# Field-pair products on one core: loads moved to ScalarE's queue, stores of two pairs from three tiles

## The chip, the cores and the metric

The kernel runs on one core of a Trainium2 chip. The metric is device time in microseconds (us) of one execution. The engines are named as the profile names them: PE (TensorE matmul) and PEld (its weight load), DVE (VectorE), ACT (ScalarE), POOL (GpSimd) and SP (SyncE), whose only work here is to issue DMAs. A "q" behind an engine's name (SPq, ACTq) marks its instruction queue.

## The reference

```python
# inputs: r_inputs [1024, 32, 128], W [496, 128, 128], all float32
pairs = list(itertools.combinations(range(32), 2))          # 496 pairs (i, j), i < j
v_i = inputs[:, I_IDX, :]
v_j = inputs[:, J_IDX, :]
transformed = jnp.einsum('bpd,ped->bpe', v_i, W)
return transformed * v_j                                    # [1024, 496, 128]
```

As the subscripts stand, each pair p has a 128x128 matrix; field i's 1024 vectors go through it, and the result is multiplied element by element with field j's vectors. 260 MB of results go to HBM, and 49 MB of inputs and weights come from it.

## The kernel before, in words

The host only reorders: `xt` is [128 (d), 32 fields, 1024 samples], `wt` holds the matrices in 62 chunks of eight pairs (`WL` = 8), and the output is [496 pairs / `OG`, 128 (e), `OG`, 1024 samples]. Pairs are visited from field i = 30 down to 0 and j from i + 1 to 31, so that few fields are needed at the start.

A pair is worked in two halves of 512 samples (`HB`); such a half is a unit u, 992 in all. For the first 15 pairs (`nq0`, i from 30 to 26) `first(u)` is one plain float32 matmul from the raw weights. From there on the operands are split into high and low parts: `split_w(c)` cuts four pairs' weights (one ACT instruction on L92, three POOL instructions on L93 to L95) and `split_x(f, a)` half a field (L106 on ACT, L107 to L109 on POOL). Then `first(u)` is two matmuls (L148) and a scaling of the PSUM tile by ACT (L149). `second(u)` adds a third matmul (L157), and DVE multiplies the PSUM tile with field j into the output tile `ot` (L163).

One loop at the end writes out the order by hand (`manual_schedule`). At step u it does, in this order: every 16 units `load_w` of the chunk two ahead (`WLEAD`); at certain pairs `load_x` of two fields that are needed later (`XLEAD`); `first(u)`; `second(u - 3)` (`LAG` = 3); and at each odd u at most one split from the list `todo`, which is sorted by due time. Each engine runs its own instructions in this order. PSUM has 8 tiles `po`, so that PE can be at most eight units ahead of DVE.

The DMAs in question:

- **Stores.** Each pair has an `ot` tile of 4 KB in each partition, from a pool of six (L64, L162). After its second half SP issues the store of 512 KB (L167). The last two pairs go out in four halves (L165).
- **Weight loads** (L83): chunks of 512 KB, 4 KB in a row, into a pool of three tiles; all issued by SP. `load_w(4)` and those after it take over a tile that earlier splits on POOL, or matmuls, have read, and wait for these.
- **Field loads** (L74): fields 30 and 31 in four halves on ACT's queue, fields 29 and 28 and the pair 26/27 by SP before the loop, and from the loop 13 loads of two fields (1024 KB, rows of 8 KB), from 24/25 down to 0/1, all by SP.

SP handles its DMAs in program order, so a load in the loop stands between the stores of the pairs around it. The framework gives the DMAs eight semaphores in rotation in program order: a DMA also waits until the eighth one before it has landed.

Of the kernel before, what the change touches and what calls it, by code (L numbers as in the profile page):

```python
# [1 line left out]

# [4 lines left out]

F32 = mybir.dt.float32
F32R = mybir.dt.float32r
ALU = mybir.AluOpType  # L10

P = 128
NF = 32
NQ = NF * (NF - 1) // 2
BT = 1024
HB = 512
WC = 4
WL = 8
OG = 1
EPS = 2.0**-12  # L20
NATIVE = 5
LAG = 3
WLEAD = 2
XLEAD = 4


def _pairs():

    return [(i, j) for i in range(NF - 2, -1, -1) for j in range(i + 1, NF)]


@with_exitstack
def kernel(
    ctx: ExitStack,
    tc: tile.TileContext,
    xt: bass.AP,
    wt: bass.AP,
    out: bass.AP,
):

    nc = tc.nc
    pairs = _pairs()
    nchunk = NQ // WC

    xpool = ctx.enter_context(tc.tile_pool(name="x", bufs=1))  # L60
    spool = ctx.enter_context(tc.tile_pool(name="xs", bufs=2))
    rpool = ctx.enter_context(tc.tile_pool(name="wr", bufs=3))
    wpool = ctx.enter_context(tc.tile_pool(name="ws", bufs=3))
    opool = ctx.enter_context(tc.tile_pool(name="o", bufs=6))  # L64
    ppool = ctx.enter_context(tc.tile_pool(name="ps", bufs=8, space=bass.MemoryType.PSUM))

    x_sb = {}

    def load_x(f, n=1, pieces=1, eng=None):

        t = xpool.tile([P, n, BT], F32, tag=f"x{f}", name=f"x_{f}")
        s = BT // pieces
        for k in range(pieces):
            (eng or nc.sync).dma_start(out=t[:, :, k * s : (k + 1) * s], in_=xt[:, f : f + n, k * s : (k + 1) * s])  # L74
        for k in range(n):
            x_sb[f + k] = t[:, k, :]

    w_raw = {}

    def load_w(c, splits=(0, WL)):  # L80
        w_raw[c] = rpool.tile([P, WL, P], F32, tag="w", name=f"w_{c}")
        for a, b in zip(splits, splits[1:]):
            nc.sync.dma_start(out=w_raw[c][:, a:b, :], in_=wt[c, :, a:b, :])  # L83

    w_s = {}

    def split_w(c):

        k = c * WC % WL
        raw = w_raw[c * WC // WL][:, k : k + WC, :].rearrange("p q e -> p (q e)")  # L90
        h, l, d = [wpool.tile([P, WC * P], F32R, tag=t, name=f"{t}_{c}") for t in ("wh", "wl", "wd")]
        nc.scalar.mul(h, raw, 1.0 - 2.0**-13)  # L92
        nc.gpsimd.tensor_tensor(l, raw, h.bitcast(F32), ALU.subtract)  # L93
        nc.gpsimd.tensor_scalar(d, h.bitcast(F32), EPS, 1.0, ALU.mult, ALU.mult)  # L94
        nc.gpsimd.tensor_tensor(d, l.bitcast(F32), d.bitcast(F32), ALU.subtract)  # L95
        w_s[c] = (h, l, d)

    x_s = {}

    def split_x(f, a):  # L100

        if a == 0:
            x_s[f] = [spool.tile([P, BT], F32R, tag=t, name=f"{t}_{f}") for t in ("xh", "xl", "xd")]
        s = slice(a, a + HB)
        h, l, d = [t[:, s] for t in x_s[f]]
        nc.scalar.mul(h, x_sb[f][:, s], 1.0 - 2.0**-13)  # L106
        nc.gpsimd.tensor_tensor(l, x_sb[f][:, s], h.bitcast(F32), ALU.subtract)  # L107
        nc.gpsimd.tensor_scalar(l, l.bitcast(F32), 1.0 / EPS, 1.0, ALU.mult, ALU.mult)  # L108
        nc.gpsimd.tensor_tensor(d, h.bitcast(F32), l.bitcast(F32), ALU.subtract)  # L109

    nq0 = NATIVE * (NATIVE + 1) // 2
    c0 = nq0 // WC
    first_q = {i: q for q, (i, j) in reversed(list(enumerate(pairs)))}

    todo = []
    for c in range(c0, nchunk):
        todo.append(((c - 2) * WC + 1, max(c * WC, nq0), lambda c=c: split_w(c)))
    for i in range(NF - 2 - NATIVE, -1, -1):  # L120
        for a in range(0, BT, HB):
            todo.append((first_q[i + 1] + 1 if i < NF - 3 - NATIVE else 2, first_q[i], lambda i=i, a=a: split_x(i, a)))
    todo.sort(key=lambda t: t[1])

    load_w(0, (0, 1, WL))
    load_x(NF - 2, pieces=2, eng=nc.scalar)
    load_x(NF - 1, pieces=2, eng=nc.scalar)
    load_x(NF - 3)
    load_x(NF - 4)
    load_w(1)  # L130
    load_x(NF - 6, 2)


    ctx.enter_context(tc.manual_schedule())
    po, ots = {}, {}


    def first(u):
        q, h = divmod(u, 2)
        i, c = pairs[q][0], q // WC  # L140
        r = slice(q % WC * P, (q % WC + 1) * P)
        s = slice(h * HB, (h + 1) * HB)
        po[u] = ppool.tile([P, HB], F32, tag="po", name=f"po_{u}")
        if q < nq0:
            nc.tensor.matmul(po[u], w_raw[q // WL][:, q % WL, :], x_sb[i][:, s], start=True, stop=True)  # L145
        else:
            for t in (0, 1):
                nc.tensor.matmul(po[u], w_s[c][t][:, r], x_s[i][t][:, s], start=t == 0, stop=t == 1)  # L148
            nc.scalar.mul(po[u], po[u], 1.0 + EPS)  # L149

    def second(u):
        q, h = divmod(u, 2)
        i, j = pairs[q]
        r = slice(q % WC * P, (q % WC + 1) * P)
        s = slice(h * HB, (h + 1) * HB)
        if q >= nq0:
            nc.tensor.matmul(  # L157
                po[u], w_s[q // WC][2][:, r], x_s[i][2][:, s], start=False, stop=True, skip_group_check=True
            )
        g, k = divmod(q, OG)  # L160
        if k == 0 and h == 0:
            ots[g] = opool.tile([P, OG, BT], F32, tag="ot", name=f"ot_{g}")  # L162
        nc.vector.tensor_tensor(ots[g][:, k, s], po.pop(u), x_sb[j][:, s], ALU.mult)  # L163
        if q >= NQ - 2:
            nc.sync.dma_start(out=out[g, :, k, s], in_=ots[g][:, k, s])  # L165
        elif k == OG - 1 and h == 1:
            nc.sync.dma_start(out=out[g], in_=ots[g])  # L167

    for u in range(2 * NQ + LAG):
        q = u // 2  # L170
        if u % (2 * WL) == 0 and (q // WL + WLEAD) * WL < NQ:
            load_w(q // WL + WLEAD)
        if u < 2 * NQ:
            i, j = pairs[q]
            if u % 2 == 0 and j == i + 1 and i % 2 == 0 and 0 <= i - 2 - XLEAD:
                load_x(i - 2 - XLEAD, 2)
            first(u)
        if u >= LAG:
            second(u - LAG)
        if u % 2 == 1:  # L180
            ready = [t for t in todo if t[0] <= q]
            if ready:
                ready[0][2]()
                todo.remove(ready[0])
    assert not todo


# [25 lines left out]
```

## Time and profile before

| | |
|---|---|
| time, median of 8 runs | 781.26 us (779.21 to 783.45) |
| the profiled execution: its own time, its span | 779.21 us, 777.4 us |
| granted TensorE clock | 0.983 of full |
| PE / DVE / ACT / POOL busy | 711.0 / 631.2 / 617.1 / 549.7 us |
| HBM read / written | 49.28 / 260.05 MB |
| DMA packets | 83730, mean 399 GB/s |

The span runs from the first to the last instruction of the profiled execution; its own time is 1.8 us more. Busy times are those of one engine and overlap with the others'. Every DMA of this kernel is spread over 16 DMA engines, each of which moves eight of the 128 rows as one packet for a row and then sends a 4-byte packet for the semaphore. A transfer has landed when all 16 have done so. "Issue to landing" counts from the issue instruction to the last of the 16.

### The profile page before, as it was taken

The page shows a single profiled execution, that of the slowest core. Times are in us where ns is not written, and L with a number is a line of the kernel's source. Part 1 is how long each engine was busy: PE and PEld are TensorE (multiplying, and loading weights), DVE is VectorE, ACT ScalarE, POOL GpSimd, SP SyncE. Part 2 cuts the span into 40 slices and gives each one's busy share as a digit, 9 for nine tenths or more (in the row PEclk, how much of TensorE's full clock was granted, in tenths as well). Part 3 has the DMA queues.
Part 4 walks back from the last instruction along what each step waited for, and adds up shares of the span by engine and source line. Part 5 has one row for each costly group of instructions (what it writes and reads, how often), then busy time and mean ns, then how long its engine had stood idle before and what let it go on. Part 6 is the DMA issues. An engine that isn't in the chain of part 4 may idle for free.

```text
span 777.4 us, 11576 instructions
## 1 busy us (share of the span) xinstructions
PE 711.0 (91%) x2946; PEld 554.5 (71%) x2946; DVE 631.2 (81%) x992; ACT 617.1 (79%) x1136; POOL 549.7 (71%) x523
## 2 busy tenths in 40 slices
PE   7889889898998989998997999899999999999994
PEld 3477668686786867777775777677777777777773
DVE  4678769687897978878886898788988888889886
ACT  1289669797986987887886888688888888888883
POOL 0999898878687885876867586667676758585550
PEclk9999999999999999999999999999999999999998
DMA  9999999999999999999999999999999999999997
GB/s 354 419 379 414 408 377 396 398 407 394 413 410 407 411 404 418 392 405 412 410 399 395 388 397 389 402 408 395 395 414 400 397 403 399 408 408 396 406 415 314
DMA packets 83730, 310.10 MB, mean 399 GB/s; under 512 B 9296, under 2 KB 9424, under 8 KB 81872
## 3 DMA queue, kind: packets, MB, share of 16 engines
q1 hardware_dynamic: 83088, 308.32, 100.4%
q10 hardware_dynamic: 576, 1.05, 0.4%
q8 instruction: 23, 0.38, 0.2%
q14 instruction: 43, 0.35, 0.1%
HBM read 49.28 MB, written 260.05 MB: 398 GB/s over the span
## 4 chain that ended last, share of the span: by engine, by line
DMA 55%; DVE 22%; PE 19%; POOL 2%; issue 1%; DVEq 0%; SPq 0%; ACT 0%; POOLq 0%
DMA out_dram<-ot 52%; DVE ot L163 22%; PE po L148 13%; PE po L157 6%; DMA x<-in_xt_dram 2%; POOL xd L109 1%; POOL xl L107 1%; DMA w<-in_wt_dram 1%; DVEq L163 0%; POOL xl L108 0%; POOL wl L93 0%; SPq L83 0%; POOL wd L95 0%; ACT xh L106 0%; POOL wd L94 0%
## 5 line engine op out<-in xcount | busy, mean ns | idle before, releaser
L163 DVE TENSOR_TENSOR ot<-po,x 128x512 f32<-128x512 f32 x992 | 631.2, 686 | 139.1 <-DMA out_dram<-ot 105.2
L149 ACT ACTIVATE po<-po 128x512 f32<-128x512 f32 x962 | 539.5, 581 | 133.2 <-PE po L148 76.3
L148 PE MATMUL po<-xh,wh 128*128 128x512 f32 x962 | 385.9, 401 | 48.6 <-DVE ot L163 48.4
L148 PE MATMUL po<-xl,wl 128*128 128x512 f32 x962 | 379.6, 395 | 3.8 <-POOL wl L93 3.1
L157 PE MATMUL po<-xd,wd 128*128 128x512 f32 x962 | 378.3, 394 | 0.0
L93 POOL TENSOR_TENSOR wl<-w,wh 128x512 fp32r<-128x512 f32 x121 | 156.1, 1290 | 155.7 <-ACT wh L92 155.6
L148 PEld LDWEIGHTS po<-xh,wh 128*128 128x128 f32 x962 | 182.6, 190 | 113.9 <-DVE ot L163 74.7
L157 PEld LDWEIGHTS po<-xd,wd 128*128 128x128 f32 x962 | 183.0, 190 | 39.7 <-ACT po L149 0.4
L148 PEld LDWEIGHTS po<-xl,wl 128*128 128x128 f32 x962 | 182.8, 190 | 39.3 <-POOL wl L93 3.5
L95 POOL TENSOR_TENSOR wd<-wl,wd 128x512 fp32r<-128x512 f32 x121 | 156.4, 1292 | 10.1
L107 POOL TENSOR_TENSOR xl<-x,xh 128x512 fp32r<-128x512 f32 x52 | 67.2, 1292 | 22.5 <-ACT xh L106 22.5
L94 POOL TENSOR_SCALAR wd<-wh 128x512 fp32r<-128x512 f32 x121 | 74.8, 619 | 10.2
L92 ACT ACTIVATE wh<-w 128x512 fp32r<-128x512 f32 x121 | 75.7, 626 | 0.0
L109 POOL TENSOR_TENSOR xd<-xh,xl 128x512 fp32r<-128x512 f32 x52 | 67.0, 1289 | 4.3
L106 ACT ACTIVATE xh<-x 128x512 fp32r<-128x512 f32 x52 | 32.6, 630 | 14.0 <-DMA x<-in_xt_dram 14.0
L108 POOL TENSOR_SCALAR xl<-xl 128x512 fp32r<-128x512 f32 x52 | 32.2, 619 | 4.5
L145 PE MATMUL po<-x,w 128*128 128x512 f32 x60 | 27.9, 626 | 4.1 <-DMA x<-in_xt_dram 4.1
L145 PEld LDWEIGHTS po<-x,w 128*128 128x128 f32 x60 | 11.6, 198 | 19.7 <-issue 12.8
L106 ACT ACT_TABLE_LOAD x1 | 1.3, 1283 | 2.6 <-issue 2.6
L200 POOL MEMSET const-float32-0.0<- 128x1 f32 x1 | 0.1, 98 | 0.2 <-issue 0.2
L200 POOL MEMSET const-bfloat16-1.0<- 128x1 bf16 x1 | 0.1, 101 | 0.0
L200 POOL MEMSET const-uint8-127<- 128x1 uint8 x1 | 0.1, 101 | 0.0
(1 smaller groups left out, 0.1 us busy)
## 6 DMA issues: line engine op xcount, KB each, us to landing
out_dram<-ot SPq DMA_DIRECT2D x494, 512.0 KB, 7.6
w<-in_wt_dram SPq DMA_DIRECT2D x61, 512.0 KB, 7.2
x<-in_xt_dram SPq DMA_DIRECT2D x14, 1024.0 KB, 10.1
x<-in_xt_dram ACTq DMA_DIRECT2D x4, 256.0 KB, 5.6
x<-in_xt_dram SPq DMA_DIRECT2D x2, 512.0 KB, 6.8
out_dram<-ot SPq DMA_DIRECT2D x4, 256.0 KB, 6.1
w<-in_wt_dram SPq DMA_DIRECT2D x1, 448.0 KB, 4.5
w<-in_wt_dram SPq DMA_DIRECT2D x1, 64.0 KB, 3.1
```

The lines of the kernel that those rows point to most:

```text
L92: nc.scalar.mul(h, raw, 1.0 - 2.0**-13)
L93: nc.gpsimd.tensor_tensor(l, raw, h.bitcast(F32), ALU.subtract)
L94: nc.gpsimd.tensor_scalar(d, h.bitcast(F32), EPS, 1.0, ALU.mult, ALU.mult)
L95: nc.gpsimd.tensor_tensor(d, l.bitcast(F32), d.bitcast(F32), ALU.subtract)
L106: nc.scalar.mul(h, x_sb[f][:, s], 1.0 - 2.0**-13)
L107: nc.gpsimd.tensor_tensor(l, x_sb[f][:, s], h.bitcast(F32), ALU.subtract)
L109: nc.gpsimd.tensor_tensor(d, h.bitcast(F32), l.bitcast(F32), ALU.subtract)
L145: nc.tensor.matmul(po[u], w_raw[q // WL][:, q % WL, :], x_sb[i][:, s], start=True, stop=True)
L148: nc.tensor.matmul(po[u], w_s[c][t][:, r], x_s[i][t][:, s], start=t == 0, stop=t == 1)
L149: nc.scalar.mul(po[u], po[u], 1.0 + EPS)
L157: nc.tensor.matmul(po[u], w_s[q // WC][2][:, r], x_s[i][2][:, s], start=False, stop=True, skip_group_check=True)
L163: nc.vector.tensor_tensor(ots[g][:, k, s], po.pop(u), x_sb[j][:, s], ALU.mult)
```

## The change

`OG` goes from 1 to 2 and the pool of output tiles from six to three: an `ot` tile now holds two pairs, 8 KB in each partition, and is stored by one DMA of 1024 KB after its fourth unit. The output array is [248, 128, 2, 1024], so that each row of a store is 8 KB in one piece. The bytes of the pool and of the output are the same. The last two pairs still go out in four DMAs of 256 KB.

The loads in the loop (60 of weights, 13 of fields) are issued by ACT on its own queue in place of SP. What is loaded before the loop stays where it was: `eng` says so at each call.

```diff
-OG = 1
+OG = 2
...
-    opool = ctx.enter_context(tc.tile_pool(name="o", bufs=6))
+    opool = ctx.enter_context(tc.tile_pool(name="o", bufs=3))
...
     def load_x(f, n=1, pieces=1, eng=None):
...
-            (eng or nc.sync).dma_start(out=t[:, :, k * s : (k + 1) * s], in_=xt[:, f : f + n, k * s : (k + 1) * s])
+            (eng or nc.scalar).dma_start(out=t[:, :, k * s : (k + 1) * s], in_=xt[:, f : f + n, k * s : (k + 1) * s])
...
-    def load_w(c, splits=(0, WL)):
+    def load_w(c, splits=(0, WL), eng=None):
...
-            nc.sync.dma_start(out=w_raw[c][:, a:b, :], in_=wt[c, :, a:b, :])
+            (eng or nc.scalar).dma_start(out=w_raw[c][:, a:b, :], in_=wt[c, :, a:b, :])
...
-    load_w(0, (0, 1, WL))
-    load_x(NF - 2, pieces=2, eng=nc.scalar)
-    load_x(NF - 1, pieces=2, eng=nc.scalar)
-    load_x(NF - 3)
-    load_x(NF - 4)
-    load_w(1)
-    load_x(NF - 6, 2)
+    load_w(0, (0, 1, WL), nc.sync)
+    load_x(NF - 2, pieces=2)
+    load_x(NF - 1, pieces=2)
+    load_x(NF - 3, eng=nc.sync)
+    load_x(NF - 4, eng=nc.sync)
+    load_w(1, eng=nc.sync)
+    load_x(NF - 6, 2, eng=nc.sync)
...
-        if q >= NQ - 2:
+        if q >= NQ - OG:
             nc.sync.dma_start(out=out[g, :, k, s], in_=ots[g][:, k, s])
         elif k == OG - 1 and h == 1:
             nc.sync.dma_start(out=out[g], in_=ots[g])
```

## The prediction, made before the changed kernel ran

> **What bounds the kernel now.** I read the page's engine rows, its DMA rows and its chain first, then the table of waits, then the DMA answer for single stretches.
>
> ```profile
> PE 711.0 (91%) x2946; PEld 554.5 (71%) x2946; DVE 631.2 (81%) x992; ACT 617.1 (79%) x1136; POOL 549.7 (71%) x523
> ...
> DMA packets 83730, 310.10 MB, mean 399 GB/s; under 512 B 9296, under 2 KB 9424, under 8 KB 81872
> ...
> q1 hardware_dynamic: 83088, 308.32, 100.4%
> ...
> DMA 55%; DVE 22%; PE 19%; POOL 2%; issue 1%; DVEq 0%; SPq 0%; ACT 0%; POOLq 0%
> ```
>
> The DMA engines are busy from end to end (100.4%: neighbouring packets overlap by 3 to 4 ns in the records), and the chain that ended last is mostly stores. The waits say the same:
>
> ```profile
> POOL wl L93 <- ACT wh L92: 155.6, 67, 4.7
> DVE ot L163 <- DMA out_dram<-ot: 105.2, 65, 5.0
> ACT po L149 <- PE po L148: 76.3, 69, 4.2
> ...
> PE po L148 <- DVE ot L163: 48.4, 48, 3.6
> ...
> PEld po L157 <- ACT po L149: 0.4, 1, 0.4
> ```
>
> DVE waits for an output tile, PE for DVE. ACT is waited for once, for 0.4 us. SP's own table has 459.3 us of waiting for DVE: its issue slots are no limit. Yet PE is close behind: between 500 and 700 us it is busy 95.5% of the time, ACT 86.1%.
>
> Two stretches give prices: 23 to 29 us moves stores alone, 594 to 600 us has a weight load among them.
>
> ```profile
> DMA packets 691, 2.52 MB, mean 420 GB/s; under 512 B 76, under 2 KB 76, under 8 KB 691
> ```
> ```profile
> DMA packets 634, 2.31 MB, mean 384 GB/s; under 512 B 71, under 2 KB 71, under 8 KB 634
> ```
>
> At 420 GB/s a transfer of 524,288 bytes takes 1.248 us. The DMA answer for 500 to 735 us has 160 stores and 20 weight loads: 180 x 1.248 = 224.6 of 235 us. The other 10.4 us are 0.52 us for each load beyond its own bytes.
>
> **Larger packets.** In the packet records a 4 KB packet takes 159 ns and its successor starts 155.3 ns after it; for 8 KB it is 309 and 306 ns, for a semaphore packet 6 ns. A 1 MB store is 8 x 306 + 6 = 2.454 us on each engine, two of today's are 2.496. That spares 0.042 us x 247 = 10.4 us, if the DMA stays the bound. The row that shows 8 KB packets is that of the field loads (14 x 128 of the 1858 packets of 8 KB and more); stores with such rows are not in the trace. Bounds: 0 if writes to HBM set the pace, 10.4 if it is the packet. I take 10.4, as 4 KB loads and stores show the same 159 ns.
>
> The Trainium skill bears on this: "DMA: Bandwidth & Descriptors", section "Rules for kernel authors", wants at least 1 MiB in a DMA, and its section "Anatomy of one DMA" gives 2.0 us fixed for each (on GpSimd's path). By that alone 247 fewer DMAs would spare an estimated 494 us. The stores-only row (420 GB/s at 512 KB) contradicts it here: fixed parts lie beside other transfers.
>
> **Loads on ACT's queue.** 60 weight and 13 field loads leave SP, which gains nothing (459.3 us spare). Each becomes an instruction of ACT:
>
> ```profile
> L83 SPq DMA_DIRECT2D w<-in_wt_dram x63: 328/667/1104, 0.7 to 735.0; - x63
> ```
> ```profile
> L74 SPq DMA_DIRECT2D x<-in_xt_dram x16: 424/1112/1487, 1.6 to 478.7; - x16
> ```
>
> (ns: least, median, most.) At the least it is 60 x 0.328 + 13 x 0.424 = 25 us, by medians 54 us, at most 86 us; ACT goes from 617 to between 642 and 703 us. Behind the issue stand the scaling (L149) of the next units and the splits, and for the scaling waits PE's third matmul. The cover is the lag of three units (a PE unit is 0.68 us, so 2.0 us) against an issue and a split (0.626 us) in a row, and PE's idle time: eight pairs take 11.75 us (235 / 20) and PE needs 16 x 0.68 = 10.9 us. I cost the issues at nothing; uncovered, 54 us. In a queue of their own loads also no longer stand in line behind stores; as the DMA engines are the bound, this moves bytes about but removes none.
>
> The skill's section "Issuing engines are not separate DMA queues" on the same page says so too: issuing from several engines saves sequencer time only. The sum would be the same by it, except that it leaves ACT's cost out.
>
> **The start.** `load_w(4)` waits for a split on POOL: SP waited 6.1 us for it (POOL wl L93), until 39.64 us. Now ACT waits, while its scalings began at 36.89 us: up to 2.8 us late, and PE and DVE with it, while the DMA ran dry (0.94 busy between 40 and 45 us). Against this, the load of fields 24/25 (issued at 6.11, landed at 17.85 us) no longer stands behind 2 MB of SP's loads, and POOL's chain could begin 2 us earlier. Bounds -2 to +2.8, taken +1. Other moved loads reuse tiles that were read long before, and the eighth DMA back is a store that must have landed for DVE to be where ACT's position implies: no wait.
>
> **Three tiles for six.** This is what the change may cost. Today, without queueing, a tile's round is 1.30 us of filling (two DVE instructions), 0.15 us to the issue, and 2.48 us from issue to the arrival from the fastest engine (least over all stores, from the sixteen semaphore arrivals of each): 3.9 us. Six stores keep an engine busy for 7.5 us: a cushion of 3.6 us. Changed: 2.60 + 0.15 + 2.48 + 1.21 (the longer data) = 6.4 us against 3 x 2.454 = 7.4: a cushion of 0.9 us, or 2.2 when a weight load (1.25 us) falls into the round. The cushion is used now: from 500 to 735 us the last of the 16 arrivals comes 2.4 us after the ninth (median). Engines that met slow load packets fall behind, the others work ahead; with a short cushion they idle, and each load's delay on the worst engine counts instead of the mean. Bounds for the 73 moved loads: nothing, to the same 0.52 us once more, 38 us. I take what the spread exceeds the cushion by in a load's round, 2.4 - 2.2 = 0.2 us: 73 x 0.2 = 14.6 us.
>
> **The sum.** -10.4 + 0 + 1 + 14.6 = +5.2 us on the span of 777.4: 782.6; 1.8 us around it: 784.4. The profiled execution (779.21) lies 2.05 us under the median of the runs: 786.4 us. A change below 0.2% (1.6 us) can't be told from none here.
>
> **The rivals.**
> - *The cushion suffices.* For it: even 0.9 us is positive, and loads arrive as extra work just when they disturb. Against it: the spread of 2.4 us. 781.26 - 10.4 + 1 = 771.9 us; with part of the 38 us of load stretches gone, since loads now mix with stores, down to 765. It wins while the cushion costs under 7.8 us, 0.11 us a load. Chance 0.36.
> - *It cancels*, cushion cost 7.8 to 11: 780 to 782.8, so 781.3 us. Chance 0.09.
> - *ACT holds PE up.* PE has 0.85 us spare in eight pairs; an issue over that (the longest was 1.10) makes PE the bound: 62 x 0.25 = 16 us for weights, and 13 x 1.49 = 19 us for field loads with nothing spare beside them, and no gain from packets: 781.3 + 35 + 1 = 817 us; half of that, about 799, is likelier. For it: PE at 95.5%. Against it: ACT's first four issues took 0.41 to 0.45 us on an empty queue. Chance 0.12.
> - *The change not doing what it says* (8 KB rows cut in two) is excluded by the field loads' packets.
>
> **How the numbers follow.** The forecast, 0.43, is the short cushion: from 782.8 up to 781.26 - 10.4 + 1 + 38 = 810. Slower is this and the third rival, 0.55. The range for 8 in 10 starts at 768, leaving out the rival's luckiest end, and stops at 807.
>
> **What would show it.** Right: "DVE ot <- DMA out_dram" stays the largest wait of DVE, some 42,000 data packets, 8 KB at 309 ns, the DMA's share under 100% with holes between loads, and a smaller gap from ninth to last arrival. Packets at 309 ns with the DMA full and the span near 768 would be the first rival; "PEld L157 <- ACT" growing from 0.4 to tens of us the third. If 8 KB stores take over 318 ns, the first step is wrong.

## The result, and the profile after

The changed kernel takes 792.61 us (median of 11 runs, 789.03 to 796.58) against 781.59 us (32 runs of the kernel before): a ratio of 1.0143, 95% interval 1.0124 to 1.0163. It is slower, as forecast, but by 11 us where 5 were forecast. The profiled execution took 788.23 us with a span of 786.4 us; its counterpart before had 779.21 and 777.4. Ratios leave out executions more than 1.5% above the fastest of the same kernel: one of six in e3, and in the kernel of e1 and e10, whose 24 executions lie between 776 and 800 us, nine of twelve and two of twelve.

The DMA rows and the chain of the page after:

```profile
DMA packets 48156, 310.03 MB, mean 394 GB/s; under 512 B 5344, under 2 KB 5472, under 8 KB 14688
...
q1 hardware_dynamic: 37008, 263.21, 81.3%
q10 hardware_dynamic: 11088, 46.14, 17.4%
...
DMA 42%; PE 30%; DVE 22%; POOL 4%; issue 1%; DVEq 0%; ACT 0%; ACTq 0%; POOLq 0%
```

The packets fell from 83730 to 48156 and 33,468 of them now have 8 KB or more: the change did what it says. The two queues together fill 98.7% of the DMA engines' time where one filled 100.4%, and the mean rate fell from 399 to 394 GB/s though the packets are cheaper. PE's share of the chain rose from 19 to 30%: over more of the span it was not a store that was waited for, but the next product.

The table of waits after:

```profile
DVE ot L163 <- DMA out_dram<-ot: 107.2, 63, 4.9
...
ACT po L149 <- PE po L148: 77.1, 69, 10.9
PE po L148 <- DVE ot L163: 51.7, 50, 3.4
DVE ot L163 <- PE po L157: 25.6, 27, 2.2
...
PE po L157 <- ACT po L149: 0.9, 1, 0.9
...
PEld po L157 <- ACT po L149: 0.4, 1, 0.4
```

DVE still waits for stores most, and for about as long as before (105.2). What grew is DVE's wait for PE's third matmul, from 7.9 to 25.6 us; the row before was:

```profile
DVE ot L163 <- PE po L157: 7.9, 10, 1.3
```

PE hardly waits for ACT (0.9 us, its weight load 0.4). ACT's issues by line:

```profile
L83 ACTq DMA_DIRECT2D w<-in_wt_dram x60: 334/334/369, 3.9 to 744.9; - x60
```
```profile
L74 ACTq DMA_DIRECT2D x<-in_xt_dram x17: 334/335/1216, 0.7 to 486.0; - x17
```

On ACT an issue takes 0.334 us, half of what SP's weight loads took (0.667); this queue holds loads alone.

**A budget of the DMA engines** makes the kernels comparable. From the packet records of each trace, as a mean of the 16 engines: *work* is the number of packets of each size times the distance of their starts when nothing is in the way (4 KB 155.3 ns, 8 KB 306, semaphore 6); *slow* is what packets took beyond their usual duration (159 and 309 ns); *idle* is the rest of the span, less some 2.5 us of instruction fetches.

| kernel (profiled execution) | span | work | slow | idle |
|---|---|---|---|---|
| before | 777.4 | 736.3 | 28.9 | 9.8 |
| after | 786.4 | 725.4 | 41.1 | 17.6 |

The larger packets gave 10.9 us. Slow packets took 12.2 back and idle time 7.8; the sum is the 9.0 us between the two spans.

### The profile page after: what moved, and what is told of

The parts are those of the page before. It is cut to its first block, busy times and chain, and to the rows that moved or that the text cites. A ratio compares the mean times of both kernels' runs of the same rounds, so it can differ in the third digit from the quotient of the medians.

```text
span 786.4 us, 10835 instructions
## 1 busy us (share of the span) xinstructions
PE 718.4 (91%) x2946; PEld 557.5 (71%) x2946; DVE 618.1 (79%) x992; ACT 624.9 (79%) x1136; POOL 549.9 (70%) x523
## 2 busy tenths in 40 slices
DMA packets 48156, 310.03 MB, mean 394 GB/s; under 512 B 5344, under 2 KB 5472, under 8 KB 14688
## 4 chain that ended last, share of the span: by engine, by line
DMA 42%; PE 30%; DVE 22%; POOL 4%; issue 1%; DVEq 0%; ACT 0%; ACTq 0%; POOLq 0%
DMA out_dram<-ot 39%; DVE ot L163 22%; PE po L148 21%; PE po L157 10%; DMA x<-in_xt_dram 2%; POOL xl L107 1%; POOL xd L109 1%; POOL wl L93 1%; POOL wd L95 0%; POOL xl L108 0%; DVEq L163 0%; POOL wd L94 0%; ACT xh L106 0%; ACT wh L92 0%; ACT po L149 0%
## 5 line engine op out<-in xcount | busy, mean ns | idle before, releaser
L163 DVE TENSOR_TENSOR ot<-po,x 128x512 f32<-128x512 f32 x992 | 618.1, 684 | 162.2 <-DMA out_dram<-ot 107.2
L149 ACT ACTIVATE po<-po 128x512 f32<-128x512 f32 x962 | 543.7, 581 | 135.2 <-PE po L148 77.1
L95 POOL TENSOR_TENSOR wd<-wl,wd 128x512 fp32r<-128x512 f32 x121 | 156.3, 1292 | 10.1
L94 POOL TENSOR_SCALAR wd<-wh 128x512 fp32r<-128x512 f32 x121 | 74.9, 619 | 10.2
L92 ACT ACTIVATE wh<-w 128x512 fp32r<-128x512 f32 x121 | 75.8, 627 | 0.8 <-PE po L145 0.8
L109 POOL TENSOR_TENSOR xd<-xh,xl 128x512 fp32r<-128x512 f32 x52 | 66.9, 1286 | 4.3
L106 ACT ACTIVATE xh<-x 128x512 fp32r<-128x512 f32 x52 | 32.6, 630 | 10.9 <-DMA x<-in_xt_dram 10.9
L145 PEld LDWEIGHTS po<-x,w 128*128 128x128 f32 x60 | 12.0, 207 | 20.8 <-issue 14.6
```

## The experiments

Theory 1: three tiles of two pairs leave the DMA engines too little queued work (the cushion of the prediction), so that they run dry and packets get slow. Rival 2: the loads on a queue of their own do it. Rival 3: a store of 1 MB with 8 KB rows is slow in itself. All ratios are against the kernel before on the same chip.

**e1 and e10: the loads alone.**

```diff
 (the changed kernel, with)
-OG = 2                        bufs=3
+OG = 1                        bufs=6
```

> One part of the change alone: the loop's loads on ScalarE's queue, stores as before (one pair, six tiles). Theory 1 (short cushion: the loss comes from three output tiles in place of six): no change within 0.4%, 779 to 785 us, the only cost being the start, about +1 us; DVE still waits some 105 us for stores. Rival 2 (queue: loads on a queue of their own mix with the stores on every DMA engine and make packets slow, or ScalarE holds TensorE up): slower by 0.8 to 1.5%, 788 to 793 us, with the time of load packets beyond 159 ns (4 KB) and 309 ns (8 KB) well above the 28 us (mean of an engine) that before has.

> The loads on ScalarE's queue alone, once more, since the twelve runs of the first time lay between 778 and 800 us. Theory 1: 779 to 785 us. Rival 2 (queue): 788 to 793 us. If the kernel has two ways of running, both will show again.

Measured: 0.9984 (0.9957 to 1.0011), and again 0.9989 (0.9960 to 1.0018), in the profile of e10 (776.84 us) with slow packets of 24.9 and 11.4 us idle. In the executions that the ratios compare, the loads' queue alone changes nothing. But the 0.9984 rests on three executions of e1, the median of all twelve is 791.0 us (781.71 in e10), and the one profiled in e1 (797.63 us) has 39.1 us of slow packets and 18 idle, as much as the changed kernel, with six small tiles. So e1 and e10 don't settle rival 2; e2 and e6 below do. Why the executions of this kernel scatter is open.

**e2: the stores alone.**

```diff
 (the kernel before, with)
-OG = 1                        bufs=6
+OG = 2                        bufs=3
```

> The other part alone: stores of two pairs with 8 KB rows from three tiles, loads on SyncE as before. Theory 1 (short cushion): as slow as the full change or slower, 790 to 797 us, DMA engines idle for 10 us or more between 30 and 765 us. Rival 2 (queue): the packets' 10 us are gained and nothing is lost, 770 to 774 us. Rival 3 (an 8 KB store is slower in itself): 790 to 797 us too, but with 8 KB store packets over 318 ns where no load is near.

Measured: 798.09 us, 1.0238 (1.0203 to 1.0273), a little above the expected 790 to 797; slow 46.1, idle 22.8 us. So the stores alone bring a loss, and without the queue of the loads it is larger: 1.0238 against 1.0143.

**e3: four small tiles.**

```diff
-    opool = ctx.enter_context(tc.tile_pool(name="o", bufs=6))
+    opool = ctx.enter_context(tc.tile_pool(name="o", bufs=4))
```

> The kernel before with four output tiles in place of six, nothing else (4 KB rows, loads on SyncE). By the prediction's arithmetic its cushion is 4 x 1.248 - 3.9 = 1.1 us, close to the 0.9 us of the full change, and no packet is saved. Theory 1 (short cushion): slower by 2 to 3%, 797 to 804 us (the 22 us that the full change lost, without its 10 us of gain). Rivals 2 and 3 (queue; large stores): no change, 780 to 783 us.

Measured: 857.92 us, 1.0971 (1.0936 to 1.1006). No large store and no moved load is in it, so fewer tiles cost time by themselves. The waits of this kernel show where:

```profile
DVE ot L163 <- DMA out_dram<-ot: 185.9, 82, 6.2
...
PE po L148 <- DVE ot L163: 108.3, 64, 5.2
```

82 waits for a store in all, a little over one for each of the 73 loads of the loop, and 2.3 us long on the mean (185.9 / 82) where before has 1.6 (105.2 / 65). The budget: work 736.3 as before, slow 62.3, idle 52.7. The direction is theory 1's, the size is not: 77 us were lost where 16 to 23 were expected. The cushion as the prediction computes it (1.1 us here, 0.9 in the changed kernel) does not rank these two kernels. Part of the difference may be the queue, for e3 has its loads on SP; but e2, which has them there too, lost less as well (1.0238).

**e4: each pair of a tile stored on its own.**

```diff
-        elif k == OG - 1 and h == 1:
-            nc.sync.dma_start(out=out[g], in_=ots[g])
+        elif h == 1:
+            nc.sync.dma_start(out=out[g, :, k, :], in_=ots[g][:, k, :])
```

> The full change, but each pair of a tile is stored on its own as soon as it is done: 512 KB DMAs, 4 KB rows, still three tiles of two pairs, loads on ScalarE. The first pair's store starts two units earlier; cushion 5 x 1.248 - 3.9 = 2.3 us in place of 0.9, the packets' 10 us not gained. Theory 1 (short cushion): 784 to 790 us, faster than the full change though its packets are small. Rival 2 (queue): the full change's loss without its gain, 800 to 804 us. Rival 3 (large stores slow in themselves): 780 to 783 us.

Measured: 788.34 us, 1.0102 (1.0078 to 1.0126). It is no slower than the full change although it gives up its gain (the intervals just touch): slow 37.5, idle 11.6, work 736.3 us. That the first pair's store starts two units earlier is worth at least about as much as the larger packets.

**e5, e6, e7: more tiles, with one load left out to make room.**

```diff
     def load_x(f, n=1, pieces=1, eng=None):
+        if f == 0:
+            x_sb[0], x_sb[1] = x_sb[2], x_sb[3]
+            return
 (e5: the changed kernel;  e6: the same with bufs=4;  e7: the kernel before with bufs=8)
```

> Control for the next run: the full change, with the load of fields 0 and 1 left out (fields 2 and 3 stand in for them), which frees 8 KB of each partition. One load of 1 MB less is some 2.5 us of DMA time plus its slow packets. All theories: 1.0 to 1.2% slower than before, 787 to 791 us.

> The control with four tiles of two pairs in the freed memory, nothing else changed. The cushion goes from 0.9 to 0.9 + 2.45 = 3.4 us, nearly the 3.6 us of six small tiles. Theory 1 (short cushion: it makes the DMA engines run dry and makes load packets slow): the packets' 10.9 us come out, 1.2 to 1.9% faster than before, 766 to 772 us; idle time of the DMA engines back from 17.6 to about 10 us and slow packets from 41 to about 29 us. Rival 2 (loads on their own queue cost): as the control less a little, 783 to 790 us. Rival 3 (large stores slow in themselves): as the control, 787 to 791 us.

> The kernel before with eight tiles of one pair and the load of fields 0 and 1 left out; cushion 8 x 1.248 - 3.9 = 6.1 us. It shows whether six small tiles were themselves short. Theory 1, if a cushion of 3.6 us covers the spread of 2.4 us: only the load left out counts, 777 to 779 us. If slow packets go on falling with a longer cushion: 768 to 774 us. Rivals 2 and 3 say nothing of it beyond 777 to 779 us.

Measured: e5 789.22 us, 1.0101 (1.0085 to 1.0116); e6 760.80 us, 0.9740 (0.9725 to 0.9755); e7 775.16 us, 0.9928 (0.9905 to 0.9951). One more tile of two pairs takes 28 us off, more than expected. The DMA rows of e5 and, below it, of e6:

```profile
DMA packets 48012, 308.98 MB, mean 392 GB/s; under 512 B 5328, under 2 KB 5456, under 8 KB 14672
```
```profile
DMA packets 48012, 308.98 MB, mean 407 GB/s; under 512 B 5328, under 2 KB 5456, under 8 KB 14672
```

The same packets, 392 and 407 GB/s. Slow fell from 39.7 to 22.6 us and idle from 22.5 to 10.6. Rivals 2 and 3 fall here: the queue and the store are the same in both. In e7 eight small tiles gain some 3 us beyond the load left out (slow 26.0). That doesn't show that six were nearly enough, for eight tiles were not free to queue up in e7. SP's own table of waits has a row there that before does not have (L169 is the store):

```profile
SPq L169 <- DMA out_dram<-ot: 238.9, 340, 2.3
```

With eight semaphores in rotation a store is issued only when the eighth DMA before it has landed, and 340 times that was another store.

**e9: four large tiles, the loads back on SP.**

```diff
 (the kernel before, load of fields 0 and 1 left out, with)
-OG = 1                        bufs=6
+OG = 2                        bufs=4
```

> Four tiles of two pairs, the load of fields 0 and 1 left out, and the other loads of the loop on SyncE as before: what the queue is worth once the cushion is long. Theory 1 (short cushion), with the queue as a side matter: 760 to 765 us, within 0.5% of the run with the loads on ScalarE (760.8 us). If the queue of their own is what keeps slow packets low (22.6 us there against 28.9 before): 766 to 772 us with slow packets near 29 us.

Measured: 767.60 us, 0.9817 (0.9796 to 0.9839); slow 28.9, idle 11.1. The second of the two expectations came true. Against e6 (0.9740) the loads' own queue is worth 0.8%, nearly all of it in slow packets: 28.9 against 22.6 us. With large tiles it helps at either length of cushion (e2 and the full change, e9 and e6). With small ones the ratios of e1 and e10 show no gain; slow packets fell there too (28.9 to 24.9 us in e10), but idle time rose (9.8 to 11.4). SP's table of e10 has two rows that bear on this:

```profile
SPq L167 <- DMA w<-in_wt_dram: 84.4, 39, 3.5
SPq L167 <- DMA x<-in_xt_dram: 23.2, 8, 4.0
```

A store needs nothing from a load, but it takes over the semaphore of the eighth DMA before it, and here that was often a load that had not landed: 107.6 us in all. In the kernel before it was 15.8 us, in those with stores of 1024 KB between 0 and 16.1 us. Whether these waits ate up the gain was not tried.

**e8 and e11: complete kernels with four large tiles.** The pool needs 8 KB more, which come from elsewhere:

```diff
 (both, from the changed kernel)
-    opool = ctx.enter_context(tc.tile_pool(name="o", bufs=3))
+    opool = ctx.enter_context(tc.tile_pool(name="o", bufs=4))
+    wpool2 = ctx.enter_context(tc.tile_pool(name="ws2", bufs=2))     # holds wl and wd
 (e8)
-    rpool = ctx.enter_context(tc.tile_pool(name="wr", bufs=3))
+    rpool = ctx.enter_context(tc.tile_pool(name="wr", bufs=2))
-        if u % (2 * WL) == 0 and (q // WL + WLEAD) * WL < NQ:
+        if u % (2 * WL) == WL and (q // WL + WLEAD) * WL < NQ:
 (e11)
-                load_x(i - 2 - XLEAD, 2)
+                if i - 2 - XLEAD:
+                    load_x(i - 2 - XLEAD, 2)
+                else:
+                    load_x(1)
+            if u == 2 * first_q[1] - 8:
+                t = rpool.tile([P, WL, P], F32, tag="w", name="x_0").rearrange("p q e -> p (q e)")
+                nc.scalar.dma_start(out=t, in_=xt[:, 0, :])
+                x_sb[0] = t
```

> A complete kernel with four tiles of two pairs. The memory comes from two raw weight tiles in place of three (each load of weights four pairs later) and two tiles each of wl and wd in place of three; the rest is the full change. Theory 1 (short cushion): 768 to 775 us, faster than both kernels, unless ScalarE or GpSimd now wait for tiles; the waits would show that. Rivals 2 and 3: 785 to 793 us.

> A second complete kernel with four tiles of two pairs, which keeps three raw weight tiles and the times of the weight loads: the memory comes from two tiles each of wl and wd in place of three, and from field 0, which is loaded late into a raw weight tile. Theory 1: the idle time at the start that the first one had (17.5 us in all) falls to about 11 us: 762 to 767 us. If GpSimd's waits for wl and wd tiles are what held the first one back: 768 to 772 us.

Measured: e8 769.84 us, 0.9862 (0.9841 to 0.9883); e11 767.95 us, 0.9812 (0.9791 to 0.9834). Both beat both kernels. The rows of e11, and its waits (its lines stand one lower: L94 and L95 are the POOL instructions for wl and wd, L149 and L158 the matmuls, L164 the product):

```profile
PE 713.4 (93%) x2946; PEld 555.0 (72%) x2946; DVE 625.9 (82%) x992; ACT 618.5 (81%) x1136; POOL 551.1 (72%) x523
...
DMA packets 48300, 310.03 MB, mean 404 GB/s; under 512 B 5360, under 2 KB 5488, under 8 KB 14960
```

```profile
POOL wd L95 <- PE po L158: 74.8, 76, 2.2
DVE ot L164 <- DMA out_dram<-ot: 69.2, 69, 3.0
...
POOL wl L94 <- PE po L149: 50.9, 35, 5.1
```

DVE's wait for stores is down from 107.2 to 69.2 us. POOL now waits for its smaller pools (74.8 and 50.9 us), and PE waits 18.1 us for POOL's L94 and L109 (10.7 and 7.4) where the changed kernel has 2.9. Slow 26.4, idle 12.6 us. e11 lies at the edge between its two expectations (762 to 767 and 768 to 772), so it doesn't tell whether POOL's waits held e8 back.

All budgets but that of e1, in us of a mean DMA engine, in the order of slow and idle together:

| kernel | output tiles x pairs | loads on | work | slow | idle | ratio |
|---|---|---|---|---|---|---|
| e6 (a load less) | 4 x 2 | ACT | 722.9 | 22.6 | 10.6 | 0.9740 |
| e10 | 6 x 1 | ACT | 736.3 | 24.9 | 11.4 | 0.9989 |
| e7 (a load less) | 8 x 1 | SP | 733.8 | 26.0 | 11.9 | 0.9928 |
| before | 6 x 1 | SP | 736.3 | 28.9 | 9.8 | 1 |
| e11 | 4 x 2 | ACT | 725.4 | 26.4 | 12.6 | 0.9812 |
| e9 (a load less) | 4 x 2 | SP | 722.9 | 28.9 | 11.1 | 0.9817 |
| e8 | 4 x 2 | ACT | 725.4 | 23.0 | 17.5 | 0.9862 |
| e4 | 3 x 2, stored by pair | ACT | 736.3 | 37.5 | 11.6 | 1.0102 |
| after | 3 x 2 | ACT | 725.4 | 41.1 | 17.6 | 1.0143 |
| e5 (a load less) | 3 x 2 | ACT | 722.9 | 39.7 | 22.5 | 1.0101 |
| e2 | 3 x 2 | SP | 725.4 | 46.1 | 22.8 | 1.0238 |
| e3 | 4 x 1 | SP | 736.3 | 62.3 | 52.7 | 1.0971 |

## Why the prediction was wrong in size and right in direction

- **Larger packets, -10.4 us: right.** Work fell by 10.9 us, and the usual 8 KB store packet took 309 ns, like the loads of before (316.8 on the mean, with the slow ones). The signs named for it (some 42,000 data packets, 8 KB at 309 ns) are there: 48156 - 5344 = 42,812. So are three others: "DVE ot <- DMA out_dram" is DVE's largest wait, the DMA's share is under 100%, and the gap from the ninth to the last arrival shrank.
- **ACT's issues, nothing: right.** 60 x 0.334 + 13 x 0.335 = 24.4 us, a little under the lower bound of 25, and PE waited 0.9 us for ACT, its weight load 0.4. The third rival is refuted. (The sentence that ACT is waited for once holds for PE alone; POOL waited 155.6 us for ACT's L92, as the first row of that table says.)
- **The start, +1 us: right within its bounds.** Slow and idle time of the first 60 us rose from 5.1 to 7.1 us, 2.0 where the bounds were -2 and 2.8. The half that was to be gained failed: ACT's first split began at 18.52 us, not earlier than the 17.88 of before; and the scalings after `load_w(4)` began at 40.69, 3.8 us later than before.
- **Three tiles for six, +14.6 us: the mis-sized term.** With the start taken out it measured 18 us: slow and idle rose by 20.0 in all, slow packets by 12.2 and idle time by 7.8. The step that failed is the line "I take what the spread exceeds the cushion by in a load's round, 2.4 - 2.2 = 0.2 us". It treats the spread as a fixed demand and a load's slow packets as a fixed price. The runs show neither. The spread shrank from 2.4 to 0.67 us (last arrival after the ninth, stores from 500 to 740 us), though the prediction itself names a smaller gap as a sign; with four large tiles it was 3.0 to 3.2 us (e11, e6). With 0.67 us the same line would have charged nothing, so that 14.6 came near 18 is luck. And slow packets depend on how much is queued: in the table above, with the same loads but for the one left out in some runs, they cost 22.6 to 28.9 us with long queues and 37.5 to 62.3 with short ones. (The one profiled in e1, 39.1 us with six small tiles, doesn't fit, and stays open.) I had put a load's price once more into the upper bound (38 us) and then took a number from the spread of the old profile. The runs support about 0.25 us for a moved load (18.0 / 73) in place of 0.2.
- **The rest of the miss.** The sum was -10.4 + 1 + 14.6 = +5.2; between the profiled executions it was +9.0, and the medians differ by 11.0, since the profiled execution of the changed kernel lies 4.4 us under its median and that of before 2.4. The terms explain 9 of the 11 us; the last two are a difference of runs that no profile here resolves. The forecast was a small difference of two large terms: 3.4 us too little for the tiles and 1.0 for the start, less the 0.5 that the packets gained beyond the forecast, make 3.9 of the 5.8 us by which the medians miss it.
- **The first rival** (the cushion suffices) is refuted by e2 and e6 together: the gain it promised comes out with a fourth tile and not with three. The second (it cancels) is refuted by the ratio, whose interval starts at 1.0124.
- **What the cushion lacks** is open in one point. By its formula e3 (1.1 us) should have lost as much as the changed kernel (0.9 us), but slow and idle rose by 76.3 us, about four times as much; in e2, which like e3 has the loads on SP, they rose by 30.2. One thing the formula leaves out can be read from the rows: between loads the DMA is faster than PE (a tile of two pairs takes 2.454 us to store and 4 x 0.68 = 2.72 us to compute), so the cushion also drains by 0.27 us a tile until the next load. This was not tried by itself, and it does not tell e3 from the changed kernel. What makes a packet slow is open as well: the runs show how much time it takes and with how many tiles, but not why.
- **The Trainium skill's rule on issuing engines** ("DMA: Bandwidth & Descriptors", "Issuing engines are not separate DMA queues": only sequencer time is saved) agrees with e1 and e10, 0.9984 and 0.9989. With two-pair tiles the measurements differ from it: e6 against e9, and the full change against e2, are 0.8 to 0.9% apart though SP waited 557.6 us (e9) and 629.4 us (e2) for DVE. The measurement decides; e9's and e6's slow packets (28.9 and 22.6 us) show where it lies, and why is not shown: on SP a load also stands in line behind stores that wait for DVE, and that was not tried apart from the queue.

## What to carry to other kernels

Where the DMA engines are the bound, the depth of the queue in front of them is part of the price: count how many buffers are really in flight while one is filled, and treat the same bytes in fewer, larger buffers as a loss until a run shows otherwise. Larger rows are worth having (1.5% of the DMA work here), and they paid once a fourth tile was found, 0.9812 in place of 1.0143. When a cushion shrinks, don't take load penalties from the old profile; they grow too. And count the semaphores: with eight in rotation, eight tiles were not free to be all in flight (e7).

## What the runs showed of the hardware

- Short queues make packets slow, not only engines idle: with nothing changed but the number of output tiles, time beyond the usual packet durations was 22.6 us of a mean engine with four large ones (e6) and 39.7 with three (e5), 28.9 with six small ones (before) and 62.3 with four (e3). In the changed kernel 4 KB load packets took 197.9 ns on the mean at a median of 159, and 8 KB stores 316.8 at a median of 309.
- An issue of 512 KB on ACT's queue took 0.334 us, on SP's queue behind stores 0.383 us (e2, three large tiles), 0.667 us (before, six small) and 1.05 us (e9, four large), all medians. So the price of an issue depends on the stores in its queue; that it waits for room there is a reading, not shown.
